# Graph attention with residual norms on one core: twelve exponential tiles instead of eleven, fewer query, key and value tiles, and later starts for the next graph's projections

## The chip, the cores and the metric

The kernel runs on one core of a Trainium2 chip. The metric is the device time of one execution in microseconds (us), as the median of several runs; lower is better.

## The reference, cut to what matters

Eight graphs share one mask of 2048 x 2048 (adj). Each graph has 2048 nodes of 256 channels, 8 heads of 32 channels. The layer is masked attention, a residual norm, a two-layer feed-forward with residual norm, and a last norm around the graph's own input.

```python
qkv = einsum('fnc,ck->fnk', x, w_qkv); q, k, v = split(qkv, 3)      # 8 heads of D=32
scores = einsum('fnhd,fmhd->fhnm', q, k) / sqrt(D)
scores = where(adj > 0, scores, -1e9)
t = einsum('fhnm,fmhd->fnhd', softmax(scores), v)
y = layernorm(x + t)                      # with ln1_g, ln1_b
z = layernorm(y + relu(y @ w1 + b1) @ w2 + b2)   # with ln2_g, ln2_b
out = layernorm(x + z)
```

## The kernel before, in words

All of it is written out by hand in one function, `fast_path`. There is no loop at run time: the order of the instructions on each engine is the order in which this Python code emits them, and each engine works its own list strictly in that order.

**Items.** The attention is cut into 8 x 128 = 1024 items (f, qc, g, mb): graph f, chunk qc of 512 queries, group g of four heads, block mb of 128 keys. Within a graph I number them n = 32 qc + 16 g + mb, from 0 to 127. An item takes four steps on four engines:

- `scores`: TensorE multiplies keys by queries for four heads (L230) into two of three PSUM pairs; VectorE reads each pair, adds the mask and writes half of an exponential tile `p` of 128 x 2048 fp32 (L233, two instructions an item);
- `exponentials`: ScalarE takes the exponential of the whole tile in place (L237);
- `values`: TensorE multiplies the tile with the values of the key block (L249), added up in PSUM over the 16 blocks of a group;
- `add_up`: the row sums for the softmax need the sum of the 16 tiles of a group. Blocks 3, 6, 8, 11, 13, 15 are added to block 0 by GpSimd (L271). Blocks 4, 7, 10 are added to block 1, and 5, 9, 12 to block 2, by accumulating DMAs that GpSimd issues (L268). Block 14 stays alone.

The item loop emits at step t: some fill work (below), the exponential of item t+1, the scores of item t+2, the values of item t and its `add_up`.

**Buffers.** The tiles `p` come from a pool `pp` of 11. A tile of a block that was added to another is free when that add has read it: at the end of a L271, or at the landing of a L268 DMA. The four tiles that hold the sums (blocks 14, 1, 2, 0) are free only when `denominator`, some steps into the next group, has multiplied them with ones (L310, four times 8 matmul passes, in that order, one in each step). The pool hands out buffers in the order in which they were released in the program, so the first L233 of an item waits for one certain earlier release, whether or not another buffer is free. Queries (`qp`, two tiles a chunk of queries), keys (`kp`) and values (`vp`, a tile a chunk and group each, 8 of each a graph) have pools of their own: 6, 12 and 12.

**Fill.** All other TensorE work is put between the items by a small planner, `advance`: generators wait in a list `fill` sorted by due step, and each step may run one unit of 4 x 512 columns (or four transposes) of the most urgent one, and more if a unit has come due. The generators are `turn` (transpose a chunk of the next graph's input and store it), `ask` (load a transposed chunk, compute its queries), `project` (load it, compute keys and values), `denominator`, `outcome` (divide, add the residual by a DMA) and `tail` (norms on VectorE, GpSimd and ScalarE, feed-forward). Loaded inputs come from a ring of three tiles, `ld`, handed out in turn: a generator can only load when the oldest is free, and a more urgent one that is blocked blocks those behind it. A load is used five steps after its issue at the earliest.

`NEXT` says at which step n of a graph each `turn`, `ask` and `project` is put into the list; for all but `ask` 1 to 3 it is the next graph's. The due step is fixed by the item that needs the result and does not depend on `NEXT`.

```python
    NEXT = {1: [(turn, 0)], 2: [(ask, 1)], 20: [(turn, 1)], 34: [(ask, 2)], 40: [(project, 0, 0)], 50: [(turn, 2)],
            60: [(project, 1, 0)], 66: [(ask, 0), (ask, 3)], 72: [(turn, 3)], 80: [(project, 2, 0)], 92: [(project, 3, 0)],
            100: [(project, 0, 1)], 104: [(project, 1, 1)], 108: [(project, 2, 1)], 112: [(project, 3, 1)]}
```

GpSimd's list holds, in item order, the adds L271, the issues of the L268 DMAs (each of a chain waits until the one before it has landed), and the parts of the norms: L282 to L286, L355, L357, L412, L414 and two residual DMAs (L334, L359). SyncE's list (SP) holds the loads of inputs (`in`), of mask pieces and the stores.

Of the kernel before, what the change touches and what calls it, by code (L numbers as in the profile page):

```python
# [61 lines left out]
def fast_path(ctx, tc, cst, x, adj, out, RS):  # L62
    nc = tc.nc
    F, N, C = x.shape
    NCK, TPC, MB = N // CH, CH // P, N // P
# [2 lines left out]
    dp = ctx.enter_context(tc.tile_pool(name="dp", bufs=1, space=bass.MemoryType.DRAM))  # L68
    mkp = ctx.enter_context(tc.tile_pool(name="mkp", bufs=MB // 2 + 1))
    ld = ctx.enter_context(tc.tile_pool(name="ld", bufs=LD))  # L70
    kp = ctx.enter_context(tc.tile_pool(name="kp", bufs=3 * NCK))
    qp = ctx.enter_context(tc.tile_pool(name="qp", bufs=6))
    vp = ctx.enter_context(tc.tile_pool(name="vp", bufs=3 * NCK))
    pp = ctx.enter_context(tc.tile_pool(name="pp", bufs=11))
    work = ctx.enter_context(tc.tile_pool(name="work", bufs=1))
    yp = ctx.enter_context(tc.tile_pool(name="yp", bufs=2))
    op = ctx.enter_context(tc.tile_pool(name="op", bufs=1))
# [416 lines left out]
    def ask(f, c):  # L494
# [2 lines left out]
        give(xT)  # L497

    NEXT = {1: [(turn, 0)], 2: [(ask, 1)], 20: [(turn, 1)], 34: [(ask, 2)], 40: [(project, 0, 0)], 50: [(turn, 2)],
            60: [(project, 1, 0)], 66: [(ask, 0), (ask, 3)], 72: [(turn, 3)], 80: [(project, 2, 0)], 92: [(project, 3, 0)],  # L500
            100: [(project, 0, 1)], 104: [(project, 1, 1)], 108: [(project, 2, 1)], 112: [(project, 3, 1)]}

    def begin():
        todo = deque((qc, c) for qc in range(NCK) for c in range(NCK))
# [204 lines left out]
def kernel(  # L709
# [56 lines left out]
    nc.gpsimd.memset(RS[:, 1], 1.0)  # L766

    fast_path(tc, cst, x, adj, out, RS)


# [49 lines left out]
```

## Time and profile before

| what | value |
|---|---|
| median of 3 runs | 3279.77 us (3279.57 to 3284.65) |
| profiled execution, its own time | 3279.45 us |
| its span, first to last instruction | 3277.3 us, so 2.15 us lie around it |
| mean granted TensorE clock | 0.983 |
| TensorE (PE) busy | 3112.2 us, 95% of the span |
| VectorE (DVE) busy | 2737.7 us, 84% |
| GpSimd (POOL) busy | 2591.2 us, 79% |
| ScalarE (ACT) busy | 2438.8 us, 74% |
| 384 accumulating DMAs of 1 MB | 10.5 us from issue to landing (median) |

Busy times are unions of an engine's instructions. A releaser, as in "<-DMA p<-p", is the event that ended the idle time before an instruction. Queue work such as issuing a DMA is shown as "POOLq" or "SPq", or as an instruction of its own on POOL. The profiled execution lies within 0.01% of the median, so sums made against it can be read against the median directly.

### The profile page before, as it was taken

The page shows a single profiled execution, that of the slowest core. Times are in us where ns is not written, and L with a number is a line of the kernel's source. Part 1 is how long each engine was busy: PE and PEld are TensorE (multiplying, and loading weights), DVE is VectorE, ACT ScalarE, POOL GpSimd, SP SyncE. Part 2 cuts the span into 40 slices and gives each one's busy share as a digit, 9 for nine tenths or more (in the row PEclk, how much of TensorE's full clock was granted, in tenths as well). Part 3 has the DMA queues.
Part 4 walks back from the last instruction along what each step waited for, and adds up shares of the span by engine and source line. Part 5 has one row for each costly group of instructions (what it writes and reads, how often), then busy time and mean ns, then how long its engine had stood idle before and what let it go on. Part 6 is the DMA issues. An engine that isn't in the chain of part 4 may idle for free. (4 is left out here: it accounts for less than half of the span.)

```text
span 3277.3 us, 68323 instructions
## 1 busy us (share of the span) xinstructions
PE 3112.2 (95%) x28948; PEld 979.2 (30%) x28948; DVE 2737.7 (84%) x3203; ACT 2438.8 (74%) x1937; POOL 2591.2 (79%) x1357
## 2 busy tenths in 40 slices
PE   7899999999999999999999999999999999999994
PEld 4222323233332223322233323323223323332221
DVE  4888988888888888888888888888888888878994
ACT  3677878777777777777777777777778777777773
POOL 0578888888878888788887888787888788878894
PEclk8899999999999999999999999999999999999997
DMA  9688779778879788788777879878779778877773
GB/s 318 145 177 189 162 179 200 176 178 197 175 174 207 171 189 185 157 197 200 180 173 173 184 179 213 173 167 197 175 179 198 175 172 201 175 164 163 164 161 77
DMA packets 153384, 591.57 MB, mean 181 GB/s; under 512 B 15056, under 2 KB 67792, under 8 KB 103920
## 3 DMA queue, kind: packets, MB, share of 16 engines
q0 software_dynamic: 64560, 435.85, 66.4%
q1 hardware_dynamic: 87696, 149.98, 13.1%
q8 instruction: 229, 3.75, 0.4%
q10 hardware_dynamic: 816, 1.31, 0.1%
q14 instruction: 83, 0.68, 0.1%
HBM read 146.67 MB, written 37.75 MB: 56 GB/s over the span
## 5 line engine op out<-in xcount | busy, mean ns | idle before, releaser
L233 DVE TENSOR_TENSOR p<-s,mask 128x1024 f32<-128x1024 f32 x2048 | 2409.4, 1218 | 395.7 <-PE s L230 190.0
L237 ACT ACTIVATE p<-p 128x2048 f32<-128x2048 f32 x1024 | 1956.2, 1910 | 554.8 <-DVE p L233 486.8
L271 POOL TENSOR_TENSOR p<-p 128x2048 f32<-128x2048 f32 x382 | 1824.0, 4776 | 268.5 <-ACT p L237 266.2
L230 PE MATMUL s<-qT,kT 32*128 32x512 f32 x8192 | 1173.5, 642 | 70.2 <-DVE p L233 65.7
L249 PE MATMUL x<-p,v 128*32 128x512 f32 x8192 | 1097.6, 608 | 14.0 <-ACT p L237 14.0
L268 POOL DMA_DIRECT2D p<-p x384 | 360.0, 955 | 289.4 <-DMA p<-p 94.4
L230 PEld LDWEIGHTS s<-qT,kT 32*128 32x128 f32 x8192 | 321.1, 183 | 679.0 <-DVE p L233 632.4
L249 PEld LDWEIGHTS x<-p,v 128*32 128x32 f32 x8192 | 161.5, 108 | 795.2 <-issue 294.2
L310 PE MATMUL x<-p,ones 128*32 128x512 f32 x2016 | 262.8, 598 | 4.3 <-POOL p L271 2.7
L54 PE MATMUL x<-in,wqkv 128*32 128x512 f32 x1888 | 244.0, 594 | 4.0 <-DMA in<-xd 4.0
L289 ACT ACTIVATE y<-y,nb,rs 128x256 f32<-128x256 f32 x372 | 219.1, 590 | 37.1 <-POOL nb L286 37.1
L278 DVE BATCH_NORM_STATS2 st<-y 128x6 f32<-128x256 f32 x372 | 155.0, 417 | 6.2 <-DMA y<-in_x_dram 6.2
L54 PE MATMUL x<-w2s,hT 128*32 128x256 f32 x2048 | 123.9, 383 | 3.2 <-DVE y L436 2.1
L54 PE MATMUL x<-turned,w1s 128*32 128x512 f32 x992 | 122.9, 592 | 0.2
L54 PEld LDWEIGHTS x<-wqkv,in 128*32 128x32 f32 x3584 | 102.3, 110 | 62.8 <-issue 59.8
L54 PE MATMUL x<-wqkv,in 128*32 128x128 f32 x3584 | 117.0, 273 | 0.0
L310 PEld LDWEIGHTS x<-p,ones 128*32 128x32 f32 x2016 | 65.7, 111 | 160.3 <-issue 145.8
L54 PEld LDWEIGHTS x<-in,wqkv 128*32 128x32 f32 x1888 | 61.3, 110 | 145.8 <-issue 112.1
L283 POOL TENSOR_TENSOR rs<-rs,mhalf 128x4 f32<-128x4 f32 x93 | 97.1, 1044 | 7.8
L54 PEld LDWEIGHTS x<-w2s,hT 128*32 128x32 f32 x2048 | 66.4, 111 | 77.0 <-issue 30.0
L414 POOL TENSOR_TENSOR y<-y,be1b2r 128x1024 f32<-128x1024 f32 x32 | 85.5, 2671 | 0.6
L355 POOL TENSOR_TENSOR y<-y,g2r 128x1024 f32<-128x1024 f32 x31 | 82.3, 2656 | 1.8 <-ACT y L289 1.8
(117 smaller groups left out, 1335.7 us busy)
## 6 DMA issues: line engine op xcount, KB each, us to landing
p<-p POOLq DMA_DIRECT2D x384, 1024.0 KB, 10.5
in<-xd SPq DMA_DIRECT2D x87, 512.0 KB, 10.6
mask<-md SPq DMA_DIRECT2D x248, 128.0 KB, 8.3
y<-in_x_dram POOLq DMA_DIRECT2D x62, 512.0 KB, 8.3
p<-in_adj_dram SPq DMA_DIRECT2D x16, 1024.0 KB, 9.5
out_dram<-y SPq DMA_DIRECT2D x31, 512.0 KB, 5.8
in<-in_x_dram SPq DMA_DIRECT2D x29, 512.0 KB, 15.3
xd<-in SPq DMA_DIRECT2D x28, 512.0 KB, 11.1
```

Of the source, the lines that this page charges most:

```text
L54: nc.tensor.matmul(out[r:r + D], lhsT[:, r:r + D], rhs, start=start, stop=stop)
L230: nc.tensor.matmul(ps2[half][:, j, :], KT[f, mb // TPC, g][r:r + D, (mb % TPC) * P:(mb % TPC + 1) * P], QT[f, qc, g][r:r + D, :], start=Tr ...
L233: nc.vector.tensor_tensor(pt[:, 2 * half:2 * half + 2, :], ps, MK[f, qc, mb // 2][:, mb % 2, None, :].to_broadcast([P, 2, CH]), ALU.add)
L237: nc.scalar.activation(PT[item], PT[item], AF.Exp, scale=1.0 / math.sqrt(D))
L249: nc.tensor.matmul(O[grp][r:r + D, :], V[f, mb // TPC, g][:, mb % TPC, r:r + D], PT[item][:, h, :], start=(mb == 0), stop=(mb == LAST))
L268: nc.gpsimd.dma_start(PT[f, qc, g, chain[0]], PT.pop(item), accum_op=ALU.add)
L271: nc.gpsimd.tensor_tensor(first, first, PT.pop(item), ALU.add)
L278: nc.vector.bn_stats(st, t[:, j, :])
L283: nc.gpsimd.tensor_tensor(rs, rs, cst["mhalf"], ALU.pow)
L289: nc.scalar.activation(t[:, j, :], t[:, j, :], AF.Identity, bias=nb[:, j:j + 1], scale=rs[:, j:j + 1])
L310: nc.tensor.matmul(ps[r:r + D, :], cst["ones"], term[:, h, :], start=(n == 0), stop=(n == len(terms) - 1))
L414: nc.gpsimd.tensor_tensor(y, y, rows(cst["be1b2r"]), ALU.add)
```

## The change

One exponential tile more, and one tile of keys, one of values and two of queries fewer: 8 KB of each partition more, and 2 + 2 + 4 KB less, so the memory used stays the same. Four entries of `NEXT` go later by 4 steps (the projections of the second group), `project` 3 of the first group goes from step 92 to 100, and `ask` 0 (the next graph's first queries) from 66 to 98. Nothing else differs: no instruction is added, removed or resized.

```diff
-    kp = ctx.enter_context(tc.tile_pool(name="kp", bufs=3 * NCK))
-    qp = ctx.enter_context(tc.tile_pool(name="qp", bufs=6))
-    vp = ctx.enter_context(tc.tile_pool(name="vp", bufs=3 * NCK))
-    pp = ctx.enter_context(tc.tile_pool(name="pp", bufs=11))
+    kp = ctx.enter_context(tc.tile_pool(name="kp", bufs=3 * NCK - 1))
+    qp = ctx.enter_context(tc.tile_pool(name="qp", bufs=4))
+    vp = ctx.enter_context(tc.tile_pool(name="vp", bufs=3 * NCK - 1))
+    pp = ctx.enter_context(tc.tile_pool(name="pp", bufs=12))
...
-            60: [(project, 1, 0)], 66: [(ask, 0), (ask, 3)], 72: [(turn, 3)], 80: [(project, 2, 0)], 92: [(project, 3, 0)],
-            100: [(project, 0, 1)], 104: [(project, 1, 1)], 108: [(project, 2, 1)], 112: [(project, 3, 1)]}
+            60: [(project, 1, 0)], 66: [(ask, 3)], 72: [(turn, 3)], 80: [(project, 2, 0)], 98: [(ask, 0)], 100: [(project, 3, 0)],
+            104: [(project, 0, 1)], 108: [(project, 1, 1)], 112: [(project, 2, 1)], 116: [(project, 3, 1)]}
```

## The prediction

> **What bounds the kernel now.** I read the engine shares first, then the table of stretches, then the list of waits, then the timeline at the places where TensorE stops.
>
> ```profile
> PE 3112.2 (95%) x28948; PEld 979.2 (30%) x28948; DVE 2737.7 (84%) x3203; ACT 2438.8 (74%) x1937; POOL 2591.2 (79%) x1357
> ...
> 1000.00:1500.00 500.00, 489.29 (x4556) 152.15 (x4552) 430.14 (x500) 388.03 (x310) 412.23 (x214) 1.00 0.83 186
> ```
>
> The second line's columns are the stretch, its length and the busy time of PE, PEld, DVE, ACT, POOL. In a steady stretch PE works 489 of 500 us: it is the bound, and 200 to 3000 us hold only 62.6 us of idle PE. No buffer count shortens PE's work, so a gain can only come from this idle time and from matmuls that run slowly after it. Who causes it:
>
> ```profile
> DVE p L233 <- DMA p<-p: 49.0, 35, 3.1
> ...
> POOL p L268 <- DMA p<-p: 94.4, 36, 6.1
> ...
> PE s L230 <- DVE p L233: 65.7, 94, 2.5
> ```
>
> PE's largest wait is for L233 (total us, times, longest us). L233 in turn waits 49 us for an accumulating DMA: the buffer that the new tile is to take has not been released. The same places return in every graph. Item 116 of graph 3, DVE and PE:
>
> ```profile
> 1607.70 1.04 PE L310 MATMUL x<-p,ones 128*32 128x512 f32 x8
> 1609.55 2.36 DVE L233 TENSOR_TENSOR p<-s,mask 128x1024 f32<-128x1024 f32 x2 [2.30 <-DMA p<-p]
> 1610.83 1.29 PE L230 MATMUL s<-qT,kT 32*128 32x512 f32 x8 [2.09 <-DVE p L233]
> 1612.04 1.94 PE L249 MATMUL x<-p,v 128*32 128x512 f32 x8
> 1613.75 1.71 PE L310 MATMUL x<-p,ones 128*32 128x512 f32 x8
> ...
> 1617.35 1.04 PE L310 MATMUL x<-p,ones 128*32 128x512 f32 x8
> ```
>
> L233 stands 2.30 us, PE 2.09 us, and then the next 24 matmul passes take 4.63 us in place of 3.00 (first start to last end). A stall of about 2 us so costs up to 3.7.
>
> **The Trainium skill.** "Perfetto Trace Analysis", Optimization Strategy, says that the same gap repeating on the engine that should be saturated can mean that no memory was left for the next tile. The trace agrees: items 24, 50, 82, 114 and 116 stall in graphs 1 to 6, with few exceptions, and each time L233 starts 0.12 us after the landing of one DMA. "TensorE: Matmul & The Clock Gate", Part 1, says that the array falls to half its clock after an idle window of about 3.4 us, and that the window runs freely. The slow passes look like that, but came after gaps of 1.88 to 2.47 us, in five places; similar gaps elsewhere (2.05, 2.54) cost nothing more. The same page says under "Architectural detail" that GpSimd takes its work strictly in order; 94.4 us of POOL waiting at L268 with adds queued behind agrees.
>
> **The change, part by part.**
>
> *Twelve tiles.* Buffers go out in the order of release. With eleven, the k-th tile takes the (k-11)th release; with twelve, the (k-12)th. So every item waits for what the item before it waited for until now. I matched each L233 to its release (end of L271, landing of L268, or end of the denominator's L310) and took the slack of both: item 24 has 0.12 us on the landing of block 4 now, and would have 7.1 on the add of block 3; items 50, 82, 114: 0.12 now, 9.9, 6.7 and 5.1 then; item 116: 0.12 now, 17.9 then. The waits move one item on: item 25 would have 2.94 on block 4's DMA, less the 1.8 that it starts earlier, so about 1.1; items 51, 83 and 115 have 2.94 less 0.2 to 2.0. Only item 117 goes under: 2.80, less 1.28 and 2.30, is -0.8, of which about 0.5 us would reach PE.
>
> What PE gets, from its gaps released by L233 over all graphs:
> - item 116, six times: 11.9 us of gaps and 4 x 1.64 of slow passes = 18.5; less 6 x 0.5 for item 117: **15.5**;
> - items 24 and 114: 5.4 + 3.3 = **8.7**;
> - item 82, six gaps: 9.9, and 1.6 of slow passes once. But look at POOL and PE after it:
>
> ```profile
> 1498.52 0.88 POOL L268 DMA_DIRECT2D p<-p  x1 [4.98 <-DMA p<-p]
> 1499.11 2.69 POOL L355 TENSOR_TENSOR y<-y,g2r 128x1024 f32<-128x1024 f32 x1
> 1501.44 4.86 POOL L271 TENSOR_TENSOR p<-p 128x2048 f32<-128x2048 f32 x1
> 1505.95 2.68 POOL L357 TENSOR_TENSOR y<-y,be2r 128x1024 f32<-128x1024 f32 x1
> 1508.93 0.88 POOL L359 DMA_DIRECT2D y<-in_x_dram  x1 [0.30 <-POOL y L357]
> 1509.55 4.86 POOL L271 TENSOR_TENSOR p<-p 128x2048 f32<-128x2048 f32 x1
> ...
> 1514.46 1.07 PE L310 MATMUL x<-p,ones 128*32 128x512 f32 x8 [0.48 <-POOL p L271]
> ```
>
> POOL works without a pause from 1498.52, before the stall at 1504.7, until the add of block 15 ends at 1514.41, and the denominator's fourth term waits for it. If PE comes 1.3 us earlier it waits 1.3 us longer: a new wait replaces the old one. Only graph 6, where PE did not wait there, may keep some: **2**;
> - item 50: 4.8 us of gaps, but at item 66 PE already waits 1.1 to 2.1 us for an exponential queued behind a norm (L289) that waits for late POOL: **0**;
> - graph 0: gaps of 2.03 (item 34) and 2.54 (item 68). The first is followed by 1.59 in which L310 waits for a landing: 0. The second: **2.5**.
>
> Sum 28.7. Against it, the longer wait at item 86 (1.3 to 2.1, plus the 0.2 to 0.9 that is there) can bring slow passes of 1.64: in half of five graphs, **-4**. Net about 25 us.
>
> *Fewer keys, values, queries.* A key, value or query tile waits if the one it replaces is still read. By steps: `project` 3 replaces the tiles of chunk 0 of the first group, last read at step 99; it starts at 100. The second group's replace chunks read until 103, 107, 111, 115, and start at 104 to 116. Queries replaced by `ask` 0 are read until 93, start 98. The waiting instruction would be ScalarE's copy out of PSUM, with exponentials queued behind, and values behind those. No wait: **0**; if one came, a step (3 us) a graph, 7 times.
>
> *Later starts.* In graphs 1 to 6 PE runs `ask` 0 at 106-109, `project` 2 at 110-113, `project` 3 at 119-124 and the second group in the next graph, at 9-28: the ring of three inputs sets this, not the start. `ask` 0 loads at about 89 now. Starting at 98 it loses that place to `project` 2, which waits behind it, and takes the next, at 105. So the two swap: the same 8 units in the same 8 steps, and one of SP's two loads in the other's place in its queue. GpSimd's list, the mask loads and the denominators stay. Graph 0 has other steps, with a few free units: plus or minus 1. **0**; if a start left steps empty, those are bound by L233 (2.5 against about 2.2 us of PE), 0.3 us each, at most 8 a graph: 17 us.
>
> *Prologue.* The mask chunks use `pp` too; one more buffer lets a load go earlier, but they land 3 to 20 us before use except the first ones and one: **0**, at most -0.5.
>
> The sum is made against the profiled 3279.45 us, 0.3 below the median. 3279.45 - 25 gives **3254 us**. About 0.2% (6.6 us) is what a measurement can tell from no change.
>
> **Rivals.**
> - *All gaps are kept* (POOL and the DMAs move up with PE): 18.5 + 8.7 + 11.5 + 4.8 + 4.6 = 48 us, 3231. For it: POOL waits 266 us for exponentials (88 of it once at the start), so it often follows PE. Against: the two POOL-bound places above.
> - *Nothing is kept*: what binds is the chain of accumulating DMAs (three of 10.5 us behind each other, and POOL standing 94 us for them), and the denominators wait for the same landings. 3274 to 3280. For it: at item 116 the third L310 would be ready at about 1609.8, just when the landing of 1609.4 allows. Against: 16 items take 48.6 us, the three DMAs 31.5 and their issues 2.9.
> - *Slower: a load comes late.* `ask` 0's load now goes out at step 105, five steps ahead of its use (some 14.6 us). In graph 0 PE once waited 4.0 us for a load (`in<-xd`, item 114). If that happened in each of seven graphs with slow passes after it, 7 x 5.6 = 39 against 28.7 gained: 3290. It decides once a load takes over 15 us; `in<-xd` lands after 10.6 in the median. Against: `project` 2's load has that slot now and PE doesn't wait in graphs 1 to 6.
> - *It does nothing*, if buffers went to whichever is free first: then item 24 wouldn't stand while others are free. The 0.12 us speak against it.
>
> **How the numbers follow.** Forecast, part kept (3240 to 3270): 0.52. All kept (3227 to 3240): 0.18. Nothing kept or nothing done: 0.17, of which 0.04 lies below the 0.2% bound. Slower: 0.13. That gives faster 0.74, same 0.13, slower 0.13. The range leaves out most of the slower case and the last of the best: 3229 to 3284.
>
> **What would show it.** Right: L233's wait for `DMA p<-p` falls from 49 to under 15 us, PE's for L233 from 65.7 to about 30; items 24, 114 and 116 run as their neighbours; L310's wait for POOL L271 grows from 2.7 to about 12; L249's for ACT stays at 14 or grows by 4. Wrong: L310's wait doesn't grow (more kept), or new gaps at L54 for `in<-xd` or ScalarE waits at L189 and L215 (the moved parts cost).

## The result, and the profile after

| | before | changed |
|---|---|---|
| median of 4 runs | 3279.67 us (3272.23 to 3284.65) | 3243.93 us (3242.05 to 3251.38) |
| profiled execution, its span | 3279.45, 3277.3 us | 3242.05, 3240.0 us |
| mean granted TensorE clock | 0.983 | 0.987 |

The ratio is 0.9897, 95% interval 0.9873 to 0.9922: the change saves 35.7 us by the medians, 37.4 between the two profiled executions. The forecast was 25.

The engine shares of the changed kernel:

```profile
PE 3101.0 (96%) x28948; PEld 976.0 (30%) x28948; DVE 2739.5 (85%) x3203; ACT 2435.5 (75%) x1937; POOL 2593.3 (80%) x1357
```

The same instructions take PE 11.2 us less (3112.2 before), and PE's idle time falls from 165.1 us (3277.3 - 3112.2) to 139.0 (3240.0 - 3101.0), by 26.1. So both terms of the prediction are there: gaps that close, and matmul passes that no longer run slowly after a gap. The first term is the firm one: in a second profiled execution of the changed kernel (below, "changed, once more") the idle time falls by 25.0, but PE's busy time only by 5.8. The list of waits says who let go (total us, times, longest us). Before, from PE's list:

```profile
PE x L249 <- ACT p L237: 14.0, 9, 4.9
...
PE x L54 <- DMA in<-xd: 4.0, 1, 4.0
PE x L310 <- POOL p L271: 2.7, 5, 0.9
...
PE s L310 <- DMA p<-p: 2.0, 1, 2.0
PE x L310 <- DMA p<-p: 1.6, 1, 1.6
```

Changed:

```profile
PE s L230 <- DVE p L233: 29.1, 65, 1.4
PE x L249 <- ACT p L237: 16.7, 11, 5.1
...
PE x L310 <- POOL p L271: 9.7, 6, 2.1
...
PE x L310 <- DMA p<-p: 6.1, 5, 4.2
...
PE s L310 <- DMA p<-p: 2.1, 1, 2.1
...
DVE p L233 <- DMA p<-p: 4.3, 4, 1.8
...
POOL p L268 <- DMA p<-p: 79.0, 33, 5.4
```

L233 waited 49.0 us for accumulating DMAs, now 4.3; PE's wait for L233 falls from 65.7 to 29.1: what is left are gaps of 0.4 to 0.7 us, most of which stand at the same items in the trace before. In return L310 now waits 9.7 us for GpSimd (2.7 before) and 8.2 for landings (6.1 + 2.1; 3.6 before), L249 16.7 for ScalarE (14.0). PE's wait at L54 for `in<-xd`, 4.0 us, is gone from the list.

The timeline of the changed kernel at items 116 and 117 of graph 3, the place that the prediction showed:

```profile
1588.75 1.14 PE L230 MATMUL s<-qT,kT 32*128 32x512 f32 x8
...
1591.68 1.14 PE L230 MATMUL s<-qT,kT 32*128 32x512 f32 x8
...
1594.10 1.07 PE L310 MATMUL x<-p,ones 128*32 128x512 f32 x8 [0.29 <-DMA p<-p]
1595.46 1.14 PE L230 MATMUL s<-qT,kT 32*128 32x512 f32 x8 [0.29 <-DVE p L233]
...
1590.03 2.35 DVE L233 TENSOR_TENSOR p<-s,mask 128x1024 f32<-128x1024 f32 x2
1594.18 2.35 DVE L233 TENSOR_TENSOR p<-s,mask 128x1024 f32<-128x1024 f32 x2 [1.79 <-DMA p<-p]
```

Item 116 (1590.03) starts without a wait, and L310 and L230 after it keep to 1.07 and 1.14 us (L310 took 1.71 here before). Item 117 (1594.18) inherits the wait for the landing: VectorE stands 1.79 us, but PE only 0.29, since VectorE worked ahead of it. That is the "wait moves one item on" of the prediction, seen directly.

### The profile page after: what moved, and what is told of

Read it like the earlier page. It is cut to its first block, busy times and chain, and to the rows that moved or that the text cites. A ratio compares the mean times of both kernels' runs of the same rounds, so it can differ in the third digit from the quotient of the medians.

```text
span 3240.0 us, 68306 instructions
## 1 busy us (share of the span) xinstructions
PE 3101.0 (96%) x28948; PEld 976.0 (30%) x28948; DVE 2739.5 (85%) x3203; ACT 2435.5 (75%) x1937; POOL 2593.3 (80%) x1357
## 4 chain that ended last, share of the span: by engine, by line
PE 75%; DVE 8%; POOL 5%; DMA 4%; issue 4%; ACT 2%; DVEq 0%; ACTq 0%; POOLq 0%
PE s L230 28%; PE x L249 24%; PE x L54 13%; DVE p L233 6%; PE x L310 6%; PE x L95 4%; DMA p<-p 3%; POOL p L271 2%; ACT p L237 2%; DMA mask<-md 1%; POOL y L357 1%; DVE st L278 1%; POOL y L355 0%; POOL y L414 0%; POOL y L412 0%
## 5 line engine op out<-in xcount | busy, mean ns | idle before, releaser
L233 DVE TENSOR_TENSOR p<-s,mask 128x1024 f32<-128x1024 f32 x2048 | 2410.5, 1219 | 360.3 <-PE s L230 202.9
L230 PE MATMUL s<-qT,kT 32*128 32x512 f32 x8192 | 1171.2, 641 | 34.1 <-DVE p L233 29.1
L249 PE MATMUL x<-p,v 128*32 128x512 f32 x8192 | 1092.9, 606 | 16.7 <-ACT p L237 16.7
L230 PEld LDWEIGHTS s<-qT,kT 32*128 32x128 f32 x8192 | 320.5, 183 | 637.8 <-DVE p L233 580.1
L249 PEld LDWEIGHTS x<-p,v 128*32 128x32 f32 x8192 | 161.3, 108 | 796.4 <-issue 302.6
L310 PE MATMUL x<-p,ones 128*32 128x512 f32 x2016 | 261.1, 594 | 15.9 <-POOL p L271 9.7
L289 ACT ACTIVATE y<-y,nb,rs 128x256 f32<-128x256 f32 x372 | 219.2, 590 | 46.1 <-POOL nb L286 46.1
L54 PE MATMUL x<-in,wqkv 128*32 128x512 f32 x1888 | 243.5, 592 | 0.0
L278 DVE BATCH_NORM_STATS2 st<-y 128x6 f32<-128x256 f32 x372 | 155.2, 417 | 6.2 <-DMA y<-in_x_dram 6.2
L54 PE MATMUL x<-w2s,hT 128*32 128x256 f32 x2048 | 122.8, 381 | 3.3 <-DVE y L436 2.3
L54 PE MATMUL x<-turned,w1s 128*32 128x512 f32 x992 | 122.9, 592 | 0.4 <-ACT in L166 0.4
L54 PEld LDWEIGHTS x<-wqkv,in 128*32 128x32 f32 x3584 | 102.2, 110 | 63.5 <-issue 59.0
L54 PE MATMUL x<-wqkv,in 128*32 128x128 f32 x3584 | 117.2, 273 | 0.0
L310 PEld LDWEIGHTS x<-p,ones 128*32 128x32 f32 x2016 | 64.1, 110 | 171.4 <-issue 136.0
L54 PEld LDWEIGHTS x<-in,wqkv 128*32 128x32 f32 x1888 | 61.7, 110 | 140.9 <-issue 113.7
L54 PEld LDWEIGHTS x<-w2s,hT 128*32 128x32 f32 x2048 | 66.1, 110 | 76.5 <-issue 30.3
L414 POOL TENSOR_TENSOR y<-y,be1b2r 128x1024 f32<-128x1024 f32 x32 | 85.4, 2667 | 0.6
L355 POOL TENSOR_TENSOR y<-y,g2r 128x1024 f32<-128x1024 f32 x31 | 82.7, 2668 | 1.2 <-ACT y L289 1.2
## 6 DMA issues: line engine op xcount, KB each, us to landing
p<-p POOLq DMA_DIRECT2D x384, 1024.0 KB, 10.5
```

What stands on the lines that cost most here:

```text
L54: nc.tensor.matmul(out[r:r + D], lhsT[:, r:r + D], rhs, start=start, stop=stop)
L230: nc.tensor.matmul(ps2[half][:, j, :], KT[f, mb // TPC, g][r:r + D, (mb % TPC) * P:(mb % TPC + 1) * P], QT[f, qc, g][r:r + D, :], start=Tr ...
L233: nc.vector.tensor_tensor(pt[:, 2 * half:2 * half + 2, :], ps, MK[f, qc, mb // 2][:, mb % 2, None, :].to_broadcast([P, 2, CH]), ALU.add)
L249: nc.tensor.matmul(O[grp][r:r + D, :], V[f, mb // TPC, g][:, mb % TPC, r:r + D], PT[item][:, h, :], start=(mb == 0), stop=(mb == LAST))
L278: nc.vector.bn_stats(st, t[:, j, :])
L289: nc.scalar.activation(t[:, j, :], t[:, j, :], AF.Identity, bias=nb[:, j:j + 1], scale=rs[:, j:j + 1])
```

## The experiments

Medians in us; each ratio is to runs of the kernel before on the same chip. Its medians there are 3277.1 to 3278.7 us, so rows can be set against each other within about 2 us.

| kernel | time | ratio, 95% interval |
|---|---|---|
| changed, once more | 3246.09 | 0.9905 (0.9890 to 0.9919) |
| twelve tiles alone | 3254.77 | 0.9930 (0.9917 to 0.9942) |
| the rest alone | 3274.49 | 0.9989 (0.9979 to 0.9999) |
| ten tiles | 3411.90 | 1.0417 (1.0402 to 1.0432) |
| before, without scale and shift | 3252.46 | 0.9919 (0.9904 to 0.9934) |
| changed, without scale and shift | 3217.52 | 0.9815 (0.9800 to 0.9830) |
| tail 4 steps later | 3411.08 | 1.0413 (1.0395 to 1.0431) |
| norm 1 step later | 3291.13 | 1.0039 (1.0025 to 1.0053) |
| thirteen tiles | 3258.14 | 0.9940 (0.9926 to 0.9953) |
| scale and shift on VectorE | 3474.47 | 1.0593 (1.0575 to 1.0611) |
| shift by DMA | 3331.69 | 1.0159 (1.0142 to 1.0175) |

### Which part of the change does it

Three kernels on one chip: the changed one, twelve tiles alone (the room is taken from keys and values, the order of all instructions is that of before), and everything but the twelfth tile (the order is that of the changed kernel).

```diff
# twelve tiles alone, against before
-  kp ... bufs=3 * NCK)    vp ... bufs=3 * NCK)    pp ... bufs=11)
+  kp ... bufs=3 * NCK - 2) vp ... bufs=3 * NCK - 2) pp ... bufs=12)
# the rest alone, against the changed kernel
-  pp ... bufs=12)
+  pp ... bufs=11)
```

> The changed kernel itself on the same chip, for the comparison. Theory and rivals alike: 34 to 38 us below the kernel before.

> Twelve exponential tiles alone: NEXT and the query tiles as before, ten tiles each of keys and values to make room; every engine's instructions stand in the order of the kernel before, only the buffer that each p tile takes differs. Theory (each tile waits for an earlier release): PE's wait for L233 falls from 65.7 to about 30 us and L310's for POOL rises to about 10, as in the changed kernel; the load wait of 4.0 us in graph 0 stays. Of the 37 us saved, about 30 come: 3247 to 3253. Rival (the moved starts do most of it): under 12 us saved, above 3267. Rival (ten key and value tiles make ScalarE's copies wait): ScalarE waits at L189 or L215 for PE, and the time is above 3280.

> The rest of the change alone: four query tiles, eleven of keys and values, the later starts, and still eleven exponential tiles; the instruction order is that of the changed kernel. Theory: the order in graph 0 saves the load wait of 4.0 us and fills two empty steps, graphs 1 to 6 only swap two units: 3 to 8 us saved, 3272 to 3277; items 24, 50, 82, 114 and 116 stall as before, PE's wait for L233 stays at 60 to 70. Rival (the starts do most of it): 25 us or more saved, below 3255.

In the traces, before and twelve tiles alone list the same instructions in the same order on all four engines (28948 on PE, 3203 on VectorE, 1937 on ScalarE, 1357 on GpSimd), and so do the changed kernel and the rest alone.

The waits of PE with twelve tiles alone:

```profile
PE s L230 <- DVE p L233: 29.5, 65, 1.4
...
PE x L310 <- POOL p L271: 8.9, 6, 2.1
...
PE x L54 <- DMA in<-xd: 4.1, 1, 4.1
```

and of the rest alone:

```profile
PE s L230 <- DVE p L233: 65.7, 95, 2.6
...
PE x L310 <- POOL p L271: 4.6, 6, 2.0
```

The twelfth tile by itself brings 23.2 us (3277.99 - 3254.77) and the whole shift of waits: L233 65.7 to 29.5, L310 for GpSimd up to 8.9. The rest brings 3.5 us, and its clear effects lie in two places: in graph 0 the load wait (`in<-xd`) goes, and items 112 to 127 take 5.3 us less; in graph 1, items 16 to 31 take 1.7 less. With eleven tiles the wait for L233 stays at 65.7. The two parts make 26.7 apart and 31.9 together (3277.99 - 3246.09). Both are less than I expected: 34 to 38 for the whole change, about 30 for the twelfth tile. Of the 8.7 between twelve tiles alone and the changed kernel, 5.4 and 1.7 lie in these two places in the traces; the rest isn't settled, as the runs of the rest alone spread over 16 us.

### One tile fewer

```diff
-  pp ... bufs=11)
+  pp ... bufs=10)
```

> Ten exponential tiles, all else as before: each item waits for what the item after it waits for with eleven. Read from the trace before, 166 items would then start 386 us later in sum if nothing else moved; a late item takes the next ones along, so less than half of it should reach the end. Theory: 3380 to 3480, with L233 waiting over 150 us for DMA p<-p. Rival (the pool hands out whichever buffer is free, so one more or less hardly counts): within 15 us of 3280.

The waits of VectorE and PE with ten tiles:

```profile
DVE p L233 <- DMA p<-p: 203.3, 85, 5.8
...
PE s L230 <- DVE p L233: 164.0, 111, 6.0
```

The dose goes the other way: L233 waits 203.3 us for landings (49.0 with eleven, 4.3 with twelve), and the time rises by 4.2%. Matching each L233 of the trace with eleven tiles to the release that is one further down made 386 us of lateness over 166 items; about a third of it (134 us) reached the end. I take the rest to be lateness that an item shares with the one before it; that is argued, not shown. The order of releases names the places, but its plain sum is no time.

### What holds the changed kernel at item 86

The prediction gave back item 82's gain at item 86, behind GpSimd. The changed kernel's timeline there, GpSimd and then PE:

```profile
1482.43 2.69 POOL L355 TENSOR_TENSOR y<-y,g2r 128x1024 f32<-128x1024 f32 x1
1484.76 4.87 POOL L271 TENSOR_TENSOR p<-p 128x2048 f32<-128x2048 f32 x1
1489.28 2.68 POOL L357 TENSOR_TENSOR y<-y,be2r 128x1024 f32<-128x1024 f32 x1
1492.26 0.88 POOL L359 DMA_DIRECT2D y<-in_x_dram  x1 [0.30 <-POOL y L357]
1492.88 4.86 POOL L271 TENSOR_TENSOR p<-p 128x2048 f32<-128x2048 f32 x1
...
1497.80 1.07 PE L310 MATMUL x<-p,ones 128*32 128x512 f32 x8 [1.36 <-POOL p L271]
```

GpSimd works through until block 15's add ends at 1497.74, and PE, which is earlier now, stands 1.36 us where it stood 0.48. To test the cause, both operations of the last norm (scale L355, shift L357) were left out, before and after the change; the result lacks them.

```diff
-        nc.gpsimd.tensor_tensor(z, z, rows(cst["g2r"]), ALU.mult)
-        nc.gpsimd.tensor_tensor(z, z, rows(cst["be2r"]), ALU.add)
```

> The kernel before without the scale and shift of the second norm in the tail (L355 and L357 left out, 31 times 2.66 and 2.69 us of GpSimd; the inputs have a scale of 1 and a shift of 0). GpSimd's other work keeps its order. Theory: eleven tiles still stall items 24 and 116, so most of the loss stays; PE's wait for POOL at L310 (2.7) goes, and where GpSimd was late for a DMA issue a landing comes earlier: 5 to 20 us below the kernel before. Rival (the chain of DMA landings alone makes GpSimd late): within 5 us of the kernel before.

> The changed kernel without the same two GpSimd instructions (L355 and L357 left out: scale and shift of the second norm). Theory: PE's new wait at item 86, L310 for POOL L271 (9.7 us in the changed kernel), is made by these two, which stand ahead of block 15's add: it falls under 2 us, and the time by 8 to 20 us against the changed kernel, so that the twelfth tile is worth more than the 37 us with them left in only if item 82 still stalls in the other run. Rival (that wait belongs to the landing that GpSimd waits for at L268): L310's wait for POOL stays above 7 us.

PE's waits in the changed kernel without the two:

```profile
PE s L230 <- DVE p L233: 28.8, 64, 1.4
PE x L249 <- ACT p L237: 13.4, 9, 2.5
...
PE x L310 <- DMA p<-p: 6.4, 4, 3.9
```

L310's wait for GpSimd is gone from the list, and items 80 to 95 keep 0.9 to 1.9 us in each of graphs 1 to 6 (7.9 in sum) that the real change gave back. The place and its cause are confirmed. The sum, though, is not larger: the same change is now worth 34.9 us (3252.46 - 3217.52), no more than with the two operations (35.7 in the result, 31.9 above). Without them eleven tiles lose less at the end of a graph: L233's waits at item 116 come to 9.8 us in six graphs, not 13.2, no slow passes follow, where they did in four graphs, and items 112 to 127 gain 9.5 us in place of 20.1.

Both runs are also shorter than I expected. Before, the two operations cost 25.9 us (3278.37 - 3252.46; expected 5 to 20), and in the changed kernel 28.6 (3246.09 - 3217.52; expected 8 to 20). So they cost more than this one wait, which was 9.7 to 11.2 us; where the rest lies stays open.

### Can GpSimd's list be eased?

Four attempts, all on the changed kernel. The first two only move work in time.

```diff
# tail 4 steps later, ahead of the scale
+        yield 4
         nc.gpsimd.tensor_tensor(z, z, rows(cst["g2r"]), ALU.mult)
# norm 1 step later, in every norm
-        yield 2
+        yield 3
```

> The changed kernel with the second half of each tail (L355 to the last norm) begun four steps later, so that block 15's add stands ahead of L355 and L357 in GpSimd's list; nothing is left out, and TensorE's list is the same. Theory: PE's wait for POOL at L310 falls from 9.7 to under 3 us and the slow passes after it go: 7 to 12 us below the changed kernel, 3231 to 3239. Rival (GpSimd's 5.3 us only move on and make the next adds late, so that other items wait for a buffer or L289 waits for its norm): no gain, within 4 us of the changed kernel, with the wait under another name.

> The changed kernel with one step more between a norm's last GpSimd instruction and its first ScalarE instruction (yield 2 becomes yield 3 in norm), so that ScalarE meets L289 a step later and the exponentials behind it aren't held up by late GpSimd. Theory: PE's wait at L249 for ScalarE (16.7 us, most of it at item 65) falls by 6 to 10 us, and the time by as much: 3233 to 3239. Rival (a step later the feed-forward that waits for this norm comes due with other work, and its units fall into double steps in which VectorE stands): no gain or up to 10 us slower.

The first was meant to let block 15's add pass ahead of the scale, and it did; L310 no longer waits for GpSimd. But the kernel became 165 us slower (3411.08 - 3246.09). PE's waits, and then the timeline of GpSimd, ScalarE and PE at one of the new places (lines below the edit are one higher here):

```profile
PE x L249 <- ACT p L237: 79.0, 15, 6.9
...
PE x L54 <- ACT hT L424: 34.2, 7, 6.3
```

```profile
1496.73 9.50 POOL L271 TENSOR_TENSOR p<-p 128x2048 f32<-128x2048 f32 x2
1506.32 0.19 POOL L282 TENSOR_SCALAR rs<-mv 128x4 f32<-128x4 f32 x1
...
1508.00 0.20 POOL L286 TENSOR_SCALAR nb<-nb 128x4 f32<-128x4 f32 x1
...
1508.23 0.60 ACT L289 ACTIVATE y<-y,nb,rs 128x256 f32<-128x256 f32 x1 [9.89 <-POOL nb L286]
1508.74 1.89 ACT L237 ACTIVATE p<-p 128x2048 f32<-128x2048 f32 x1
...
1510.68 1.93 PE L249 MATMUL x<-p,v 128*32 128x512 f32 x8 [6.07 <-ACT p L237]
```

A small norm operation on GpSimd (L282 to L286) stands behind two pair adds of 9.50 us together; ScalarE's L289 waits 9.89 us for it, the exponential stands behind L289, and PE 6.07 us behind that, then with slow passes (1.93). My theory fell: the wait didn't go, it moved to where more stands behind it. The second attempt gives that small operation a step more; the waits of PE and VectorE:

```profile
PE x L54 <- DVE y L436: 39.2, 15, 4.2
...
DVE y L436 <- POOL y L414: 72.4, 19, 6.5
```

L249's wait for ScalarE falls from 17.1 us (changed, once more) to 0.4, as intended, but now the feed-forward's L436 waits for GpSimd's L414: 45 us slower, more than the rival's 10. The order of TensorE's instructions moves in this run too, so the 45 us aren't put down to GpSimd alone. In both runs the wait for GpSimd only moved to another place.

The other two take work off GpSimd: scale and shift on VectorE in halves, or the shift as an accumulating DMA.

```diff
# scale and shift on VectorE
-        nc.gpsimd.tensor_tensor(z, z, rows(cst["g2r"]), ALU.mult)
-        yield 1
-        nc.gpsimd.tensor_tensor(z, z, rows(cst["be2r"]), ALU.add)
-        yield 1
+        for name, op in (("g2r", ALU.mult), ("be2r", ALU.add)):
+            for h in range(0, TPC, 2):
+                nc.vector.tensor_tensor(z[:, h:h + 2], z[:, h:h + 2], rows(cst[name])[:, h:h + 2], op)
+                yield 1
...
-        yield 7
+        yield 5
# shift by DMA
-        nc.gpsimd.tensor_tensor(z, z, rows(cst["be2r"]), ALU.add)
-        yield 1
+        nc.gpsimd.dma_start(z, rows(cst["be2r"]), accum_op=ALU.add)
+        yield 4
         nc.gpsimd.dma_start(z, xin, accum_op=ALU.add)
-        yield 7
+        yield 4
```

> The changed kernel with the last norm's scale and shift (two GpSimd operations of 2.67 and 2.68 us, 31 times each, 165.7 us) moved to VectorE in halves of 128x512, four instructions per tail at about 0.69 us (the mean of the row of L436, of the same size): 124 x 0.69 = 86 us more on VectorE; what TensorE has in each step is unchanged. Theory (what the changed kernel still waits for at item 86 is GpSimd's queue, where these operations stand ahead of the pair additions): the wait of the pairs' sum for GpSimd goes from 9.7 to about 0, as it went when the two operations were left out altogether (3217.5 us); VectorE's part delays stores at the steps concerned by up to 0.69 us each and TensorE meets some of it, 0 to 25 us: 3217 to 3242 us. Rival (VectorE is nearer to its bound than GpSimd, so that each half pushes the stores behind it and TensorE waits for L233): L233's part of TensorE's waits rises from 29 to over 60 us, 3246 us or more.

> The changed kernel with one of the two GpSimd operations of the last norm taken off it: the shift (L357, 31 times 2.68 us) becomes an accumulating DMA of the same half megabyte, whose issue costs GpSimd about 1.06 us (the row of L359), so 31 x 1.62 = 50 us less on GpSimd, with the residual's DMA 4 steps (some 12 us) later and the last norm where it was. Theory (what is left of the stall at item 86 is the time that GpSimd needs ahead of block 15's addition): 1.6 us less ahead of it takes away all but about 1 us of the 9.7 us that TensorE waits there, and some of the 28.6 us that leaving both operations out brought: 3225 to 3240 us. Rival (the accumulating DMAs are nearer to their bound: 31 more of half a megabyte among 384 of one and 62 of half come to 31 x 0.5 / 415 = 3.7% more, and a tile added by DMA then comes free later; or the second DMA's issue waits on GpSimd for the first one's landing): the waits for p<-p rise from 8.3 us at the pairs' sum and 4.3 us at L233, 3250 us or more.

On VectorE it is 6% slower than before. The timeline of VectorE, GpSimd and PE at one tail (L357 is the line of the new operation):

```profile
1573.77 4.66 DVE L357 TENSOR_TENSOR y<-y,be2r 128x512 f32<-128x512 f32 x1
...
1581.15 2.20 DVE L357 TENSOR_TENSOR y<-y,be2r 128x512 f32<-128x512 f32 x1
...
1573.02 9.78 POOL L271 TENSOR_TENSOR p<-p 128x2048 f32<-128x2048 f32 x2
...
1580.15 2.09 PE L230 MATMUL s<-qT,kT 32*128 32x512 f32 x8 [4.79 <-DVE p L233]
```

I had priced each half at 0.69 us, from L436. It takes that (median 0.68) where no pair add is running on GpSimd when it starts; but of the 124, 64 began under a running add, and every one of those ended 0.54 to 0.56 us after that add's end: the half at 1581.15 ends at 1583.35, the adds at 1582.80. Seven more, recorded as starting up to 0.5 us ahead of an add, ended 0.56 us after it as well; the other 53 took 0.69 at most, four of them begun up to 0.7 us ahead of an add. Which of two close starts came first the records don't tell. They cost 295 us in all in place of 86, TensorE stands 4.79 us behind one, and the passes that follow are slow: PE's busy time is 3184.1 us, 83 more. The Trainium skill, "SBUF — State Buffer", "SBUF: two separate sides", has this: VectorE and GpSimd share one pair of SBUF ports, a VectorE operation with two inputs in SBUF contends for it with a GpSimd operation that reads SBUF, and whoever starts first has it for its whole instruction. The 64 ends agree. L436 and L345 read one input from PSUM and keep to 0.69 us. The rival was right about the time and the wait for L233 (202.9 us), but the measured load is 295 us and not 86, and the lock is what fits the difference.

By DMA it is slower as well, for the second mechanism that the rival named. GpSimd's and VectorE's waits there:

```profile
POOL y L359 <- DMA y<-be2r: 97.0, 24, 7.6
...
DVE st L278 <- DMA y<-in_x_dram: 51.0, 14, 11.7
```

The landings took 5.6 to 18.2 us (10.5 in the median), and GpSimd mostly came to L359 earlier than that: it stood there 24 times, 97.0 us against the 50 that were to be saved, with pair adds queued behind. The residual's DMA then lands late, and VectorE stands 51.0 us for it at L278 (6.2 in the changed kernel). The saving was smaller as well: an issue took 1.64 us, not 1.06, so 31 x 1.04 = 32 us.

### One tile more by the same means

```diff
-  kp ... bufs=3 * NCK - 1) vp ... bufs=3 * NCK - 1) pp ... bufs=12)
+  kp ... bufs=3 * NCK - 3) vp ... bufs=3 * NCK - 3) pp ... bufs=13)
-            60: [(project, 1, 0)], 66: [(ask, 3)], 72: [(turn, 3)], 80: [(project, 2, 0)], 98: [(ask, 0)], 100: [(project, 3, 0)],
-            104: [(project, 0, 1)], 108: [(project, 1, 1)], 112: [(project, 2, 1)], 116: [(project, 3, 1)]}
+            66: [(ask, 3)], 72: [(turn, 3)], 98: [(ask, 0)], 100: [(project, 1, 0)], 104: [(project, 2, 0)], 108: [(project, 3, 0)],
+            112: [(project, 0, 1)], 116: [(project, 1, 1)], 120: [(project, 2, 1)], 124: [(project, 3, 1)]}
```

> The change carried on by the same means: thirteen exponential tiles, ten each of keys and values, and the next graph's projections again later, so that they fit the tiles (chunk 1 at steps 100 to 103, chunks 2 and 3 at 104 to 111, the second halves at 112 to 127). Theory (in order of items a store is late where its tile is released after VectorE could have begun; in the changed kernel's trace only 12 of 1024 items have less than 1 us left, so the wait for a tile is used up): at most 2 to 5 us less than the changed kernel from these, and what is left over is the 9.7 us at the pairs' sum for GpSimd, which no tile takes away; against that, steps 60 to 63 and 80 to 83 lose their projections and the steps 100 to 127 carry them all: between 3 us faster and 15 us slower than the changed kernel, 3243 to 3261 us. Rival (each further tile is worth as much as the twelfth was, 23 us alone): 3223 us.

It is 12 us slower than the changed kernel, so the twelfth tile's gain doesn't repeat. The waits of PE and VectorE:

```profile
PE s L230 <- DVE p L233: 43.3, 84, 2.1
...
DVE p L233 <- POOL y L414: 18.2, 6, 3.4
```

PE's wait for L233 rises from 29.1 to 43.3 us. The second line is no new wait: its six times lie at item 66, where VectorE stood 18.9 us in the changed kernel too, then put down to ScalarE's L289. Against the changed kernel's trace, items 0 to 31 lose 2.7 to 6.6 us in each of graphs 1 to 7, 28.0 in all, and items 80 to 95 win back 9.7. TensorE's busy time at L54 in these graphs grows from 179.1 to 202.3 us in items 0 to 31 and falls from 46.9 to 21.7 in items 80 to 95: the fill moved later, and crowds the start of the next graph. The run changes tiles and order together, so what a thirteenth tile alone would do stays open; L233's 4.3 us of waits for landings, in the list of the changed kernel, are what it could take away directly.

## Why the prediction was right, point by point

The savings below are from the starts of L233, in stretches of 16 items, before less after; all stretches together make 37.3 us.

- **Items 112 to 127** (116 and 114), graphs 1 to 6: predicted 15.5 + 3.3 = 18.8, measured 20.1. Matching each L233 to the release one further up gave the places. The term for item 117 was too large: it goes under in three graphs (VectorE stands 1.79, 0.84 and 0.76 us), and PE gives 0.29 us in one of them, where six times 0.5 was taken off. Without it the gaps and slow passes make 21.8; graph 3 gives 1.04 of these to a wait at L249 that no term has.
- **Items 16 to 31** (24), graphs 1 to 7: predicted 5.4, measured 7.9. Twelve tiles alone gain 6.2 there; the other 1.7 are the moved starts' in graph 1.
- **Item 50**: predicted 0, measured -0.2 over items 48 to 79 of graphs 1 to 6. The result is right, the reading of the lines was not. PE's gaps for L233 around this item are 4.0 us in these graphs, but 2.5 of them, one of 0.41 or 0.42 in each graph, stand in the changed kernel as before; only 1.5 belonged to a late tile. Items 48 to 63 win 1.2, and PE's waits for the exponential just ahead of item 66 grow from 8.4 to 9.6 us, as foreseen.
- **Item 82**: predicted 2 kept and 4 lost to slow passes, -2 net; measured over items 80 to 95 of graphs 1 to 6, -0.3. The gain was handed to L310 at item 86 in all six graphs (waits of 1.1 to 2.1 us), so the 2 that graph 6 was to keep was not kept. Slow passes followed once (graph 2: a gap of 2.11, then 4.75 us for 24 passes).
- **Graph 0**: the mis-sized step. "Plus or minus 1" for its order and 2.5 for the gap at item 68 stand against 7.1. The 2.5 was right (2.6 over items 64 to 79), but the later `ask` 0 also took away the load wait of 4.0 us and its slow passes at item 114: 5.3, shown again by the rest alone. I had named that very wait only as a risk, not asked what the new order does to it. Against this, 1.6 went the other way, at item 34, where a wait of 4.18 us for a landing is now followed by slow passes.
- **Fewer keys, values, queries: 0.** In ScalarE's list L189 and L215 wait for their own projection (L54) and for no tile in use: 100.2 us before, 91.2 changed, and 96.0 with twelve tiles alone, which has one key and one value tile less still.
- **Rivals.** *All gaps kept* (3231) fails at item 86, and the runs without scale and shift show what that place alone withholds: 7.9 us over items 80 to 95, in place of -0.3. *Nothing kept* and *does nothing* fail on 4.3 us in place of 49.0. *A load comes late* was the wrong way round: the load wait went away.

The terms of the prediction come to 24.7 us, the stretches to 37.3. Of the 12.6 between them, graph 0 is 4.6, items 16 to 31 are 2.5, item 82 is 1.7, items 112 to 127 are 1.3 and item 50 is -0.2; the last 2.7 are in no term: 1.35 in the prologue and the tail, and as much in the other stretches of graphs 1 to 7.

Part of this is luck. The second profiled execution of the changed kernel repeats the stretches 16 to 31 (7.9), 112 to 127 (20.0) and the end of graph 0 (5.3). But it has -4.4 us at items 80 to 95, where L310's wait was followed by slow passes in graphs 1, 2 and 6, and nothing at graph 0's first 16 items, which hold 1.6 of the 7.1 us. So the 4 us for slow passes were a fair guess, and the -0.3 a lucky draw. The 6.6 us of slow passes at item 116 before are such a draw too: the rest alone, which also has eleven tiles, had them in one graph of six.

## What to carry to other kernels

Where a pool hands out buffers in the order of release, one buffer more moves every wait to the release before: list the slack of each request against that earlier release, and the table says where the gain lies, where the wait will reappear, and when the next buffer is no longer worth its room. Then ask, for each place where time is won, which in-order queue comes next; here GpSimd's took back the gain of one of the five places. Before work is moved off a full queue, price it against what runs at that moment on the engine it goes to, not by a row of the same size alone.

## What the runs showed of the hardware that I had not expected

- An fp32 `tensor_tensor` of 128x512 on VectorE with both inputs in SBUF took 0.68 us, or lasted until about 0.55 us after the end of the GpSimd add beside it (up to 5.9 us). The mask add L233, with one input in PSUM, took 1.23 us at most beside the same adds.
- Slow matmul passes follow some gaps and not others of the same length (2.09 us in graph 3 before, then 4.63 us for 24 passes; 2.05 in graph 1, then 3.00), and the granted clock in the traces tells them apart. Before, between 200 and 3000 us, it falls to half at 427.26, 1219.16, 1611.69, 2004.22, 2396.76 and 2686.89 us, for 3.41 us each time. The distances are 232, 115, 115, 115 and 85 times 3.413 us, so these pieces lie on a fixed grid. Graph 3's gap lies in one piece of it (1608.28 to 1611.69), and the next has half the clock. Graph 1's is cut at 826.60, so that no piece holds more than 1.74 us of idle PE, and the clock stays. Among this trace's pieces at full clock after 100 us, those that half the clock followed held 1.88 us of idle or more, and the others at most 1.74; in the 13 traces together it followed all above 2.05 and none below 1.75. The Trainium skill, "TensorE: Matmul & The Clock Gate", Part 1, has this freely running window; it asks for an idle one of about 3.4 us, where here some 1.9 us within one sufficed. Where a gap falls on the grid changes from execution to execution, and with it whether it costs 1.64 us more.
- Delaying the second half of each tail by four steps cost 165 us, more than leaving its scale and shift out had brought (28.6). At the place shown, the delay passed through three queues behind each other: GpSimd's, ScalarE's and TensorE's.
